# Layer 3's spreading matrix: from a comparison of positions to a turned selection

## The chip, the cores and the metric

The kernel runs on one core of one Trainium2 chip. The time is device microseconds of one execution. Three runs of the kernel before took 1780.59, 1781.38 and 1783.02 us, so the median is 1781.38 us. Beside these there is one profiled execution, from which the trace is taken; it has its own time.

## The reference

A graph of 3327 nodes with 512 features goes through four layers. Each layer adds its input to its output and normalises the rows. The change touches the fourth, called layer 3, an attention layer with 4 heads of 128:

```python
h = jnp.einsum('nf,hfo->hno', x, hamilton)
f_src = jnp.einsum('hno,ho->hn', h, a_src)
f_dst = jnp.einsum('hno,ho->hn', h, a_dst)
e = jax.nn.leaky_relu(f_src[:, :, None] + f_dst[:, None, :], ALPHA)
e = jnp.where((adj > 0)[None, :, :], e, NEG_INF)
attn = jax.nn.softmax(e, axis=-1)
h_prime = jnp.einsum('hnm,hmo->hno', attn, h)
out = jnp.transpose(h_prime, (1, 0, 2)).reshape(N, -1)
return jax.nn.elu(out)
# and around it
x = _layernorm(x + _L3_gnn_ref(x, adj, L3_gnn_W, L3_gnn_a), axis=-1)
```

The adjacency is sparse except for its first rows and columns, so the kernel works on lists of edges.

## The kernel before, in words

The nodes lie in 26 blocks of 128 rows. For each block from 1 to 25 the kernel has a list of the edges that end in it, sorted so that the edges of one row lie side by side. A list is cut into chunks of 128 edges ("places"). Block 1 has 15 chunks, later blocks have fewer (6 around block 11, 5 from block 15, 4 from block 23), 165 in all. The edges from the first 128 nodes are left out of the lists and added per block as a dense product, called the column here.

One to four chunks make a group, and the function `group` handles one group. It is a Python generator, and each `yield` ends one of its stages. In layer 3, before the change, its stages are:

1. POOL starts one indirect transfer per chunk (L1005), which gathers 128 rows of 2,080 bytes from the table in device memory into a ring of 27 chunk places. ACT zeroes the weights of places that don't exist (L1253) and computes |2 x place - middle| per row (L1267, "far").
2. DVE compares it with the row's number of edges (L1277). The result "ds" is the spreading matrix: 128 rows by 128 places per chunk, 1 where the place belongs to the row.
3. PE multiplies ds with the rows' own scores, in three parts (L1291, into "pg"), so that every place gets the score of its row.
4. DVE adds the gathered score and takes the maximum (L1304, L1306, "sc"); ACT takes the exponential twice (L1307, L1308) and turns the kept selection of layer 2 from 8 bits into f32 (L1312, "sel"): 128 places by 128 rows per chunk, 1 where the place belongs to the row.
5. DVE multiplies the gathered rows by the weights (L1315).
6. PE adds sel times these rows to the block's sums in PSUM (L1334). With the last chunk goes the column's product (L1331).

The list `sall` keeps the selection that layer 2 built for all its groups, and `kept` returns a group's part of it. It is there for every block that layer 3 handles in groups. In layer 0 it isn't.

From layer 1 on the order of the instructions on every engine is the order in which the program issues them. In layer 3 that order comes from this loop:

```python
for k, item in enumerate(groups(pools[0], range(1, NB))):
    if item[4] == 0:
        ends.add(g3.column(item[0], fin))
    work.add(g3.group(item, pools, accs, layer3, sall))
    both()
```

`both` is one step: first every live group runs its next stage, the oldest first; then every live generator of the list `ends` does, the oldest first. `ends` holds two kinds. A column is added when its block's first group is added:

```python
nc.sync.dma_start(up, ...)                     # L1366
for _ in range(4):
    yield
for h in range(H):
    nc.scalar.activation(up[:, h, :], ..., AF.Relu, ...)   # L1371, ACT
yield
nc.vector.scalar_tensor_tensor(up, up, ...)    # L1373, DVE
```

So four Relus on ACT come four steps after the block's first group has been started, and DVE's product "upc" comes one step later. Three buffers hold "upc". The other kind, `layer3_end`, is added when a block's last chunk has been summed. One step later it divides by the sum of the weights (DVE "rden", L1481 and L1482; ACT "h", four instructions, L1485) and takes an exponential (ACT "e", L1495). In the step after that DVE finishes the row (L1497, L1498) and takes its moments (L802, L804), and ACT takes a logarithm and an exponential of the variance ("r", L828 and L829). In the third DVE refines it (L835 to L837, "nm" in L856), ACT scales the row ("o", L857), and SP stores it (L770).

Of the kernel before, what the change touches and what calls it, by code (L numbers as in the profile page):

```python
# [8 lines left out]
F32 = mybir.dt.float32  # L9
BF16 = mybir.dt.bfloat16  # L10
# [6 lines left out]
I16 = mybir.dt.int16  # L17
AF = mybir.ActivationFunctionType
ALU = mybir.AluOpType
AX = mybir.AxisListType  # L20
PSUM = bass.MemoryType.PSUM
DRAM = bass.MemoryType.DRAM

P = 128
# [513 lines left out]
GROUP = 4  # L538
# [93 lines left out]
def sparse_path(ctx, tc, flag_i, x, adj, l0_w, l0_a1, l0_a2, l1_w_self, l1_b_self, l1_w_nb, l1_b_nb,  # L632
# [13 lines left out]
    nc = tc.nc  # L646
# [12 lines left out]
    def pool_in(lay, name, bufs=1, **kw):  # L659
        return lay.enter_context(tc.tile_pool(name=name, bufs=bufs, reuse_waits="tile", **kw))  # L660
# [38 lines left out]
    dgs = keep.tile([P, NL, 2], F32, name="dgs")  # L699
# [10 lines left out]
    def iota(name, n, dtype, step, base, mult, pool=const):  # L710
        t = pool.tile([P, n], dtype, name=name)
        nc.gpsimd.iota(t, pattern=[[step, n]], base=base, channel_multiplier=mult,
                       allow_small_or_imprecise_dtypes=True)
        return t
# [3 lines left out]
    ident16 = const.tile([P, P], BF16, name="ident16")  # L718
# [3 lines left out]
    place = iota("place", LMAX * P, I16, 1, 0, 0)  # L722
# [45 lines left out]
    def store(dst_d, b, t, shift=0):  # L768
        for p0, p1 in rows_of(b):
            nc.sync.dma_start(dst_d[shift + b * P + p0:shift + b * P + p1, :], t[p0:p1])  # L770
# [83 lines left out]
    def scaled_by_act(o, y, fin, mv, rs):  # L854
        nm = fin.tile([P, 1], F32, name="nm")
        nc.vector.scalar_tensor_tensor(nm, mv[:, 0:1], -1.0, rs, ALU.mult, ALU.mult)  # L856
        nc.scalar.activation(o, y, AF.Identity, bias=nm, scale=rs)  # L857
# [127 lines left out]
    def groups(ring, blocks=range(NB), whole=False):  # L985


        for b in blocks:
            at = 0
            for l in lists[b]:  # L990
                c0, end = 0, l.L if whole else l.up
                while c0 < end:
                    left = end - c0
                    g = -(-left // -(-left // GROUP))
                    if ring.ahead() < g:
                        g = ring.ahead()
                    yield b, l, c0, g, at
                    c0 += g
                    at += g
# [10 lines left out]
    def kept(sall, b, at, g):  # L1010

        if sall is None or b == 0:
            return None
        at += spot[b]
        lo, t = next((lo, t) for lo, t in reversed(sall) if lo <= at)
        return t[:, at - lo:at - lo + g, :]
# [9 lines left out]
    class Gat:  # L1026
# [199 lines left out]
        def close_first(self, pool, ps, mean):  # L1226
# [11 lines left out]
            for s in range(2):  # L1238
                nc.tensor.matmul(self.acc[s], lone, G[0:1, s * hh:(s + 1) * hh, :], start=False, stop=True)

        def group(self, item, pools, accs, done, sall=None):

            b, l, c0, g, at = item
            ring, sp, pacc, pone = pools
            H, OUT, M = self.H, self.OUT, self.M
            hh = H // 2
            whole = self.k == 0
# [5 lines left out]
                nc.scalar.copy(G[p0:p0 + 32, g - 1].rearrange("p (h m) -> p h m", m=M)[:, :, OUT:],  # L1253
                               zeros[p0:p0 + 32, :2 * H].rearrange("p (h s) -> p h s", s=2))

            na = min(g, max(0, l.up - c0))
            nb = min(g, max(0, l.down - c0)) if whole else g
            far = sp.tile([P, GROUP * P], I16, name="far")
            parts = [(far, 0, 0, na), (far, 1, na, g if whole else na)]
            if nb < na:  # L1260
                more_far = sp.tile([P, 2 * P], I16, name="far1")
                assert na - nb <= 2
                parts.append((more_far, 1, nb, na))
            for t, k, q0, q1 in parts:
                if q0 < q1:
                    o = t[:, q0 * P:q1 * P] if t is far else t[:, :(q1 - q0) * P]
                    nc.scalar.activation(o, place[:, (c0 + q0) * P:(c0 + q1) * P], AF.Abs,  # L1267
                                         bias=l.nmid[:, k:k + 1], scale=2.0)
            yield
            have = kept(sall, b, at, g)  # L1270
            ds = sp.tile([P, GROUP * P], BF16, name="ds")
            for t, k, q0, q1 in parts:
                o, dk = ds[:, q0 * P:q1 * P], dgs[:, l.at, k:k + 1]
                if t is not far:
                    nc.vector.scalar_tensor_tensor(o, t[:, :(q1 - q0) * P], dk, o, ALU.is_lt, ALU.add)
                elif q0 < q1:
                    nc.vector.tensor_scalar(o, t[:, q0 * P:q1 * P], dk, None, ALU.is_lt)  # L1277
            yield

            pg = pone.tile([P, 512], F32, name="pg")  # L1280
# [3 lines left out]
            for c in range(g):  # L1284
# [5 lines left out]
                for k in range(3):  # L1290
                    nc.tensor.matmul(po, ds[:, c * P:(c + 1) * P], self.own[:, k, :, b],  # L1291
                                     start=k == 0, stop=k == 2)
            S = sp.tile([P, GROUP, P], F32, name="sel")
            if have is None:
                turned = pg[:, 256:].bitcast(BF16)
# [27 lines left out]
            for c in range(g):  # L1323
# [9 lines left out]
                for s in range(2):  # L1333
                    nc.tensor.matmul(accs[b][s], S[:m, c, :], G[:m, c, s * hh * M:(s + 1) * hh * M],  # L1334
                                     start=at + c == 0, stop=last)
# [188 lines left out]
    lay, listlay, wxlay = ExitStack(), ExitStack(), ExitStack()  # L1524
# [16 lines left out]
    with ExitStack() as pro:  # L1541
# [81 lines left out]
        ready, whole = -1, True  # L1623
# [194 lines left out]
    def both():  # L1818
        work.step()
        ends.step()  # L1820
# [9 lines left out]
    with ExitStack() as lay:  # L1830
# [6 lines left out]
        sp = pool_in(lay, "l1s", 3)  # L1837
# [120 lines left out]
    with ExitStack() as lay:  # L1958
        fin = pool_in(lay, "l2f", 2)
        sp = pool_in(lay, "l2s", 1)  # L1960
# [5 lines left out]
        g3 = Gat("g3", t3_d, H3, OUT3, w3, 1)  # L1966
# [75 lines left out]
    with ExitStack() as lay:  # L2042
        pools = (Ring(H3 * (OUT3 + 2), rows, extra), pool_in(lay, "l3s", 3),
                 pool_in(lay, "l3pa", 2, space=PSUM), pool_in(lay, "l3p1", 3, space=PSUM))
        fin = pool_in(lay, "l3f", 2)

        def layer3(b, acc):
            ends.add(layer3_end(b, acc))

        def layer3_end(b, acc):  # L2050
            yield
            e, mv, rs = yield from g3.summed(fin, acc, xres[b])
            o = fin.tile([P, D], F32, name="o")
            scaled_by_act(o, e, fin, mv, rs)
            store(out, b, o)

        def verdict():

            yield
            bad = fin.tile([P, 4, NL], F32, name="bad")  # L2060
            nc.vector.memset(bad, 0.0)
            nc.vector.tensor_tensor(bad[:, 0, :], deg[:, 1:], cnt, ALU.not_equal)
            used = fin.tile([P, 3, NL], F32, name="used")
            room = fin.tile([P, 3, NL], F32, name="room")
            nc.vector.tensor_add(used[:, 1:], starts.rearrange("p l s -> p s l"), dgs.rearrange("p l s -> p s l"))
            nc.vector.tensor_add(used[:, 0], used[:, 1], used[:, 2])
            for ls in lists:
                for l in ls:
                    for k, n in enumerate((l.room, l.near, l.far)):
                        nc.gpsimd.memset(room[:, k, l.at:l.at + 1], float(n))  # L2070
            yield
            nc.vector.tensor_tensor(bad[:, 1:], used, room, ALU.is_gt)
            tot = fin.tile([P, 2], F32, name="tot")
            nc.vector.tensor_reduce(tot[:, 0:1], bad, AX.XY, ALU.add)
            nc.vector.tensor_reduce(tot[:, 1:2], spread, AX.X, ALU.add)
            nc.vector.tensor_add(tot[:, 0:1], tot[:, 0:1], tot[:, 1:2])
            yield
            pt = pools[3].tile([P, 512], F32, name="pg")
            nc.tensor.matmul(pt[0:1, 0:1], tot[:, 0:1], ones[:, 0:1], start=True, stop=True)
            nc.vector.tensor_copy(flag_i, pt[0:1, 0:1])  # L2080

        ends.add(g3.open_column(fin))
# [5 lines that stand above are left out]
            if k == 6:  # L2088
                ends.add(layer3_end(0, bias1))
            if k == 12:  # L2090
                ends.add(verdict())
        while work.live or ends.live:
            both()


@with_exitstack
def kernel(ctx: ExitStack, tc: tile.TileContext, *args):


    nc = tc.nc  # L2100
    pool = ctx.enter_context(tc.tile_pool(name="flagp", bufs=1))
    flag_i = pool.tile([1, 1], I32, name="flag_i")
    sparse_path(tc, flag_i, *args)
    again = nc.values_load(flag_i[0:1, 0:1], min_val=0, max_val=1 << 20)
    with tc.If(again > 0):
        general_path(tc, *args)
# [30 lines left out]
```

## Time and profile before

| what | value |
|---|---|
| runs shown, median of three | 1781.38 us (1780.59 to 1783.02) |
| the profiled execution, its own time | 1689.52 us |
| the profiled span, first to last instruction | 1687.8 us |
| mean granted TensorE clock | 0.957 |
| gathers of layer 3 on POOL | 165, from 1418.1 to 1635.3 us |
| multiplication of the first and of the last group (L1315) | 1429.2 and 1662.5 us |
| busy from 1460 to 1660 us (200 us) | PE 167.1, DVE 180.8, ACT 155.3, POOL 135.2 us |

Times within the profile are counted from the span's start. A line of the timeline gives the start, the duration, the engine, the line of the kernel, the operation, what it writes and reads, and how many instructions are merged; a bracket at its end gives the engine's idle time before it and what ended that. The chain lists the work that determined the end, in order of time.

### The profile page before, as it was taken

What the parts mean: (1) busy time and instruction counts of PE and PEld (TensorE: products, weight loads), DVE (VectorE), ACT (ScalarE), POOL (GpSimd) and SP (SyncE); (2) the same over time, 40 slices, a digit from 0 to 9 for tenths busy, and PEclk for the clock granted to TensorE, in tenths of its full rate; (3) what the DMA queues carried; (4) which work ended last, traced back from release to release, by engine and by line L of the source; (5) the groups of instructions that cost most, each with busy time, mean ns of one, the idle gap of its engine ahead of it and who ended that gap; (6) DMA issues with size and microseconds to landing.
All of it is one profiled execution on the core that took longest, in us unless ns stands there. A gap on an engine that the chain in (4) does not pass through costs nothing. (4 is left out here: it accounts for less than half of the span.)

```text
span 1687.8 us, 24368 instructions
## 1 busy us (share of the span) xinstructions
PE 1490.9 (88%) x7298; PEld 994.6 (59%) x7298; DVE 1220.4 (72%) x3289; ACT 874.4 (52%) x2921; POOL 767.4 (45%) x904
## 2 busy tenths in 40 slices
PE   5979987989999989889999999787999996888884
PEld 3756655656666767445555555433566664777663
DVE  7998979988668789316556677547666644789996
ACT  5889856666666768312112221112444444568885
POOL 3000076564554620065445445047777402777750
PEclk9989989999999999879999999899999997999998
DMA  8787787776664542198888889168998613888871
GB/s 258 241 285 248 233 256 252 236 205 197 190 189 148 182 121 89 46 390 327 292 311 302 318 300 342 72 207 289 300 322 296 219 38 114 228 232 253 253 225 46
DMA packets 130401, 381.98 MB, mean 226 GB/s; under 512 B 22037, under 2 KB 36477, under 8 KB 130259
## 3 DMA queue, kind: packets, MB, share of 16 engines
q0 software_dynamic: 67696, 252.97, 46.7%
q1 hardware_dynamic: 62563, 127.35, 22.3%
q8 instruction: 60, 0.98, 0.2%
q14 instruction: 82, 0.67, 0.1%
HBM read 331.89 MB, written 48.37 MB: 225 GB/s over the span
## 5 line engine op out<-in xcount | busy, mean ns | idle before, releaser
L1005 POOL DMA_INDIRECT gl<-t_d,idx x270 | 274.2, 1015 | 221.9 <-DMA e_d<-es 80.6
L1005 POOL DMA_INDIRECT gt<-t_d,idx x201 | 203.6, 1013 | 345.2 <-DVE cand L921 198.0
L1334 PE MATMUL acc<-gt,sel 128*128 128x264 f32 (+3 forms) x804 | 208.7, 405 | 3.7 <-issue 1.8
L797 PE MATMUL po<-wn,xt 128*128 128x512 f32 x416 | 195.5, 613 | 11.6 <-ACT vc L963 4.9
L1005 POOL DMA_INDIRECT gm<-t_d,idx x136 | 136.5, 1004 | 137.9 <-PE acc L1810 87.8
L1334 PEld LDWEIGHTS acc<-gt,sel 128*128 128x128 f32 (+3 forms) x804 | 151.0, 197 | 39.6 <-issue 13.4
L1334 PE MATMUL acc<-gl,sel 128*128 128x260 f32 (+3 forms) x544 | 140.8, 405 | 27.1 <-issue 14.9
L797 PEld LDWEIGHTS po<-wn,xt 128*128 128x128 f32 x416 | 79.4, 196 | 96.7 <-issue 77.5
L1334 PEld LDWEIGHTS acc<-gl,sel 128*128 128x128 f32 (+3 forms) x544 | 102.6, 198 | 44.5 <-issue 15.6
L1315 DVE TENSOR_TENSOR gt<-gt,pg 128x1536 f32<-128x1536 f32 (+3 forms) x63 | 116.3, 1847 | 13.6 <-ACT sel L1310 13.4
L1042 PE MATMUL po<-gt,xt 128*128 128x268 f32 x416 | 111.4, 410 | 15.5 <-ACT xt L789 11.6
L785 ACT COPY xt<-pt 128x512 f32<-128x512 f32 x81 | 46.8, 588 | 132.1 <-PE pt L782 121.8
L1810 PE MATMUL acc<-gm,selr 128*128 128x512 f32 (+4 forms) x324 | 107.9, 457 | 4.5 <-DMA gm<-t_d,idx 4.1
L909 DVE MAX8 cand<-val 128x8 f32<-128x464 uint16 (+32 forms) x184 | 107.5, 619 | 0.0
L1042 PE MATMUL po<-w,xt 128*128 128x262 f32 x416 | 99.3, 392 | 5.2 <-ACT xt L789 3.9
L1042 PEld LDWEIGHTS po<-gt,xt 128*128 128x128 f32 x416 | 75.6, 195 | 34.3 <-ACT xt L789 15.5
L1267 ACT ACTIVATE far<-place,nmids 128x128 int16<-128x128 int16 (+3 forms) x167 | 88.3, 545 | 13.5 <-DVE ds L1277 12.9
L797 PE MATMUL po<-wl,xt 128*128 128x512 f32 x208 | 93.4, 594 | 0.7 <-ACT xt L785 0.7
L797 PE MATMUL po<-wx,xt 128*128 128x512 f32 x208 | 93.5, 594 | 0.0
L1042 PEld LDWEIGHTS po<-w,xt 128*128 128x128 f32 x416 | 78.9, 192 | 23.1 <-ACT xt L789 5.8
L782 PE MATMUL pt<-s_ident,xres 128*128 128x128 f32 x500 | 78.8, 287 | 14.2 <-DVE xres L852 10.0
L881 ACT ACTIVATE m<-ab 128x1664 bf16<-128x1664 int32 x50 | 80.1, 1603 | 16.8 <-DMA ab<-in_adj_dram 12.5
(372 smaller groups left out, 3225.6 us busy)
## 6 DMA issues: line engine op xcount, KB each, us to landing
ab<-in_adj_dram SPq DMA_DIRECT2D x25, 832.0 KB
ab<-in_adj_dram SPq DMA_DIRECT2D x25, 831.5 KB
t_d<-t SPq DMA_DIRECT2D x25, 512.0 KB
gm<-t_d POOLq DMA_DIRECT2D x25, 512.0 KB
t_d<-t SPq DMA_DIRECT2D x25, 384.0 KB
t_d<-tg SPq DMA_DIRECT2D x25, 264.0 KB
gd<-t_d SPq DMA_DIRECT2D x25, 264.0 KB
t_d<-tg SPq DMA_DIRECT2D x25, 260.0 KB
```

The source lines that it names most:

```text
L782: nc.tensor.transpose(pt[:, c, :], src[:, c * P:(c + 1) * P], ident)
L785: nc.scalar.copy(xt, pt)
L797: nc.tensor.matmul(po, xt[:, c, :], w[:, c], start=c == 0, stop=c == DC - 1)
L881: nc.scalar.activation(m, ab[s], AF.Sign, accum_out=half[:, s, b:b + 1])
L909: nc.vector.max(out=cand[:, s, :], in_=val[:, cuts[s]:cuts[s + 1]])
L1005: nc.gpsimd.indirect_dma_start(out=t[:m, c, :], out_offset=None, in_=table[:, :], in_offset=bass.IndirectOffsetOnAxis(ap=l.idx[:m, c0 + c: ...
L1042: nc.tensor.matmul(pw[s], xt[:, c, :], self.w[:, c, s, :], start=c == 0, stop=c == DC - 1)
L1267: nc.scalar.activation(o, place[:, (c0 + q0) * P:(c0 + q1) * P], AF.Abs, bias=l.nmid[:, k:k + 1], scale=2.0)
L1315: nc.vector.tensor_mul(Gc[:, :, :OUT], Gc[:, :, :OUT], w[:, :g].rearrange("p c (h o) -> p (c h) o", o=1).to_broadcast([P, g * H, OUT]))
L1334: nc.tensor.matmul(accs[b][s], S[:m, c, :], G[:m, c, s * hh * M:(s + 1) * hh * M], start=at + c == 0, stop=last)
L1810: nc.tensor.matmul(accs[b], chosen, parts[:, k * D:(k + 1) * D], start=at + c + k == 0, stop=k == top and at + c == n - 1)
```

## The change

In layer 3 the spreading matrix is no longer computed from the positions. PE multiplies each chunk of the kept selection (8 bits, as stationary operand) with the 128 x 128 identity, which turns it, into a PSUM tile "pd" of a new pool with one buffer. ACT copies that tile into ds as bf16. The absolute value on ACT and the comparison on DVE are left out. The group has seven stages instead of six: gather; turn on PE; copy on ACT; then stages 3 to 6 as before. The old code goes into a function of its own, `spread_own`, which layer 0 still runs, in the same order as before.

```diff
+        def spread_own(self, sp, l, c0, g, whole):
             na = min(g, max(0, l.up - c0))
             nb = min(g, max(0, l.down - c0)) if whole else g
...
                     nc.scalar.activation(o, place[:, (c0 + q0) * P:(c0 + q1) * P], AF.Abs,
                                          bias=l.nmid[:, k:k + 1], scale=2.0)
             yield
-            have = kept(sall, b, at, g)
-            ds = sp.tile([P, GROUP * P], BF16, name="ds")
+            self.ds = ds = sp.tile([P, GROUP * P], BF16, name="ds")
...
                     nc.vector.tensor_scalar(o, t[:, q0 * P:q1 * P], dk, None, ALU.is_lt)
+
+        def group(self, item, pools, accs, done, sall=None):
...
+            have = kept(sall, b, at, g)
+            if have is not None:
+                yield
+                turned = self.around.tile([P, 512], F32, name="pd")
+                for c in range(g):
+                    nc.tensor.matmul(turned[:, c * P:(c + 1) * P], have[:, c, :], ident16, start=True, stop=True)
+                yield
+                ds = sp.tile([P, GROUP * P], BF16, name="ds")
+                nc.scalar.copy(ds[:, :g * P], turned[:, :g * P])
+            else:
+                yield from self.spread_own(sp, l, c0, g, whole)
+                ds = self.ds
             yield
...
+        g3.around = pool_in(lay, "l3p0", 1, space=PSUM)
```

More of the change, by code (lines that the diff above doesn't have):

```diff
@@ L1239, in close_first @@
                 nc.tensor.matmul(self.acc[s], lone, G[0:1, s * hh:(s + 1) * hh, :], start=False, stop=True)
[L1241 to L1247, printed above, removed]
-            total = (chunks_all if whole else chunks_of)[b]
-            G = gather(ring, self.table, l, c0, g, whole)
-            m = l.places(c0 + g - 1, whole)
-            for p0 in range(m, P, 32):
-                nc.scalar.copy(G[p0:p0 + 32, g - 1].rearrange("p (h m) -> p h m", m=M)[:, :, OUT:],
-                               zeros[p0:p0 + 32, :2 * H].rearrange("p (h s) -> p h s", s=2))
+        def spread_own(self, sp, l, c0, g, whole):
             na = min(g, max(0, l.up - c0))
@@ L1277, in group @@
                     nc.vector.tensor_scalar(o, t[:, q0 * P:q1 * P], dk, None, ALU.is_lt)
+        def group(self, item, pools, accs, done, sall=None):
+            b, l, c0, g, at = item
+            ring, sp, pacc, pone = pools
+            H, OUT, M = self.H, self.OUT, self.M
+            hh = H // 2
+            whole = self.k == 0
+            total = (chunks_all if whole else chunks_of)[b]
+            G = gather(ring, self.table, l, c0, g, whole)
+            m = l.places(c0 + g - 1, whole)
+            for p0 in range(m, P, 32):
+                nc.scalar.copy(G[p0:p0 + 32, g - 1].rearrange("p (h m) -> p h m", m=M)[:, :, OUT:],
+                               zeros[p0:p0 + 32, :2 * H].rearrange("p (h s) -> p h s", s=2))
+            have = kept(sall, b, at, g)
[10 more added lines that the diff above has]
+                ds = self.ds
             yield
```

## The prediction

> **What bounds the kernel now.** I read the page's shares first, then layer 3 in stretches of 20 us, then the chain, then the timeline of single blocks. The page, and two of the stretches (busy us and instruction count of PE, PEld, DVE, ACT, POOL; granted clock; DMA share; GB/s):
>
> ```profile
> PE 1490.9 (88%) x7298; PEld 994.6 (59%) x7298; DVE 1220.4 (72%) x3289; ACT 874.4 (52%) x2921; POOL 767.4 (45%) x904
> ...
> 1600.00:1620.00 20.00, 16.30 (x111) 13.24 (x110) 18.75 (x47) 17.90 (x58) 15.43 (x16) 1.00 0.84 244
> 1640.00:1660.00 20.00, 15.98 (x104) 12.41 (x104) 18.18 (x48) 16.44 (x52) 0.00 (x0) 1.00 0.22 67
> ```
>
> Over the whole span PE looks like the bound; in layer 3 DVE (91 to 94%) and ACT (82 to 90%) are the fullest. POOL issues a gather every 1.25 us (16 in 20 us) until 1635 and is done 27 chunks before the consumer. Two regimes follow. In blocks 1 to 5 a group's product on DVE starts 4.7 to 11.9 us after its last gather was issued, at the low end waiting for data. From block 10 (1539.8) the distance is 8.3 us and it grows to 28: here the gathers are ahead and something else sets the pace. The chain says what, for one block of 3 + 2 chunks:
>
> ```profile
> 1623.12 0.51 ACT far L1267
> 1623.63 0.70 ACT o L857
> 1624.33 1.03 ACT h L1485 x4
> 1625.39 0.64 ACT e L1495
> 1626.05 0.70 DVE h L1497
> 1626.78 0.70 DVE e L1498
> 1627.50 0.70 DVE st L802
> 1628.36 1.16 DVE gl L1315
> 1631.28 0.51 ACT far L1267
> ```
>
> It is a ring through ACT and DVE, once per block, closed by sc, max, the weights and sel. No engine is full for lack of speed alone: each waits for the other inside a fixed order. I call the step in which DVE multiplies a block's first group the first step, the one with its second group the second step. The timeline of both:
>
> ```profile
> 1618.77 1.63 ACT L1371 ACTIVATE upc<-upc,low,rcol 128x128 f32<-128x128 f32 x4
> 1620.06 0.18 DVE L804 BATCH_NORM_AGGREGATE mv<-st 128x2 f32<-128x6 f32 x1
> 1620.31 0.28 ACT L828 ACTIVATE r<-mv,s_eps 128x1 f32<-128x1 f32 x1
> ...
> 1621.98 0.51 ACT L1312 ACTIVATE sel<-salla 128x384 f32<-128x384 fp8e4 x1
> 1622.49 0.61 ACT L1253 COPY gl<-zeros 32x8 f32<-32x8 f32 x3
> 1623.12 0.51 ACT L1267 ACTIVATE far<-place,nmids 128x256 int16<-128x256 int16 x1
> 1623.53 0.80 ACT L857 ACTIVATE o<-e,nm,rs 128x512 f32<-128x512 f32 x1
> ```
>
> The four Relus for the column stand in the first step, and end just when ACT's next work ("r") gets its input from DVE: they are free. In the second step ACT goes from sel to o, h and e without a gap, and DVE then waits for e.
>
> **What the Trainium skill says.** "PSUM — Partial Sum Buffer", section "Engine vs sequencer instructions": ScalarE and VectorE work their queues strictly in order. The trace agrees: where Relus stand ahead of o, o waits for them (shown below). "ScalarE: Activation LUTs", section "What ACT_TABLE_LOAD costs": an activation takes 186 ns plus 0.833 ns per element, 280 with a bias pointer, and neighbours overlap by 93 ns. The trace agrees: sel of 384 takes 506 ns, far of 384 takes 602.
>
> **The change part by part.**
>
> Removed from DVE: the comparison, in the window from 1450 us 9.4 + 3.9 + 2.5 + 0.5 = 16.3 us in 50 groups, 0.33 us each. Removed from ACT: far, 0.60 us for 384, 0.50 for 256. Added on ACT: a copy out of PSUM. The nearest row is layer 0's cast of the turned tile from PSUM, 467 ns at 128x384, and 588 ns for f32 at 128x512; the skill's price for 384 is 506, less 93 of overlap 413. I take 0.42 us from start to start for 384 (ends: 0.33 and 0.51). ACT alone would thus win about 0.1 us per group. Added on PE: one 128 x 128 turn per chunk. Layer 0's turns of the same size take 0.35 us for three in a row, so 0.12 each; 8-bit weights load in 98 ns in layer 2, so they are no dearer. For 165 chunks that is 19 us on an engine with 3 to 4 us idle in each 20. Sending the transfers costs the same: 165 gathers, in the same order on POOL, with no new DMA on any queue.
>
> The added stage is what I think decides. A group's product now comes five steps after its start, not four, while the column still counts four steps from that start to its Relus. So everything that is issued by count from the start moves one step earlier against the products, the sums and the row ends. Most blocks have two groups, so the Relus move from the first step, where they cost nothing, into the second, and there they stand ahead of o, h and e, because the column is older in the list than the row ends. DVE's upc moves into the first step, ahead of h, where DVE waits for e anyway: free. ACT's zeroing of absent places moves from the second step into the first: 0.2 to 0.6 us off the ring. Of SP's queue: the load of the next column waits for the sum that frees its buffer, now one step later relative to it; three steps (about 13 us) are left to the Relus against a few for the load, and the stores behind it on SP have two buffers: no cost.
>
> The ring before, start to start, from h at 1617.88: DVE h 0.73, e 0.73, st 0.72, mv 0.10, product of two chunks 1.11, sc 0.22, max to the weights 0.26 (1621.75), weights 0.23, sel 0.51, zeros 0.63, far 0.41, o 0.71, h 1.15, e 0.66 = 8.17 (next h at 1626.05). Over blocks 15 to 22 the mean is (1647.5 - 1583.8) / 8 = 7.97, since blocks without zeros are held by DVE's nm instead. After: without zeros and far, with the copy 0.42 and the Relus 1.54 (1618.77 to 1620.31): 8.17 - 1.04 + 1.96 = 9.1. For 3 + 3 chunks the product adds 0.54 less 0.09 of shorter waits: 9.55. For 4 + 3, sel and copy add 0.2: 9.75; for 4 + 4 the product adds 0.55: 10.3.
>
> Summed by first products (L1315): blocks 6 to 9 took 1503.97 to 1539.78 = 35.8, after 10.3 + 3 x 9.75 = 39.5: +3.7. Blocks 10 to 12 took 25.6, after 3 x 9.55 = 28.6: +3.0. Block 13 has three groups and block 14 two, 18.4 together; one of the two meets the new order: +1.0. Blocks 15 to 22: 8 x (9.1 - 7.97) = +9.0. Blocks 23 and 24, 14.9: +1.1 each, +2.2. Blocks 1 to 5 and the 25 us after the last product: 0. Sum +18.9. The span goes from 1687.8 to about 1707, the profiled execution from 1689.5 to about 1708. The runs shown are 92 us above the profiled one; nothing in layer 3 says that this part changes, so the median goes from 1781.4 to about 1800.
>
> What the kernel before shows of this order: around block 13, with its three groups, Relus fall into the step of o:
>
> ```profile
> 1580.57 0.16 DVE L856 SCALAR_TENSOR_TENSOR nm<-mv,rs 128x1 f32<-128x1 f32 x1
> 1580.61 0.60 ACT L1267 ACTIVATE far<-place,nmids 128x384 int16<-128x384 int16 x1
> 1581.12 1.63 ACT L1371 ACTIVATE upc<-upc,low,rcol 128x128 f32<-128x128 f32 x4
> 1582.66 0.80 ACT L857 ACTIVATE o<-e,nm,rs 128x512 f32<-128x512 f32 x1
> ```
>
> nm is done at 1580.73, and o starts at 1582.66, when the Relus end.
>
> The new waits: PE's turn waits for ACT's copy of the group before (one buffer), and that stands behind the weights and sel. Behind the turn on PE stand the sum of an older group and the scores of the next. In the first step the copy comes after e, some 6.2 us after the ring's max. PE then turns (0.35), sums three chunks (2.87), makes the scores (0.3) and is done at about 9.8; the addition that needs them comes at 9.1 + 2.7 = 11.8. About 2 us of cover; without it each us of delay costs a us per block. PE's own work is 5 x 0.96 + 1.05 + 0.7 + 0.6 = 7.1 of 9.1; for 4 + 4 it is 10.7, 0.4 above the ring, in one block.
>
> **The rivals.** (1) DVE relief wins, ending faster. For: DVE is at 94%, and 16.3 us leave it. If the Relus keep cover, the ring loses far minus copy (0.1 to 0.2) and part of the zeros, about 0.25 us in 16 blocks: -4, 1777. Decided by where the Relus stand: it holds if they end before mv. Against: the count of four steps is not changed. (2) PE becomes the bound: turn after copy after sel, one buffer, and the sums behind it late for the addition. From 2 us more delay than worked out above, each further us goes onto the block; with 0.5 us in 20 blocks, 1810. Against: the cover above. (3) Half of it: up to block 12 the gathers hide the longer ring, since there 7 to 8 chunks take 8.75 to 10 us of POOL. Then 1.0 + 9.0 + 2.2 = +12, 1793. Against: the distance to the gathers grows already from block 9. (4) Nothing moves, within 3 us of 1781: the Relus in the second step are made up by a DVE that is free earlier. Against: DVE waits for e there.
>
> **How the numbers follow.** Relus on the ring 0.58, half of it 0.14, PE bound 0.15, relief 0.08, nothing 0.05. The likeliest gives 1800, its own range 1794 to 1808 (copy 0.33 to 0.51 is +-2 us over 20 blocks, three-group blocks and the tail +-3). The 8-in-10 range reaches to the half case and PE's: 1787 to 1812. About 0.2%, 3.6 us, is what a measurement of this kernel can tell from no change. Faster 0.08, same 0.05, slower 0.87.
>
> **What would show it.** Right: in blocks 15 to 22 the Relus follow the copy and o follows the Relus, DVE waits over 1 us per block for e, and first products lie about 9.1 us apart; DVE's share from 1460 to 1660 falls below 85%. Wrong: the Relus still end before r; or PE's sums wait for the turn and sc waits for PE's scores (rival 2); or the multiplications up to block 12 keep their times (rival 3).

## The result and the profile after

| | before | after |
|---|---|---|
| median of 15 runs each | 1782.22 us (1773.4 to 1790.63) | 1794.8 us (1787.45 to 1802.38) |
| ratio | 1 | 1.0075, 95% interval 1.006 to 1.009 |
| predicted | 1781.4 | 1800, range 1787 to 1812 |

The change makes the kernel slower by 12.6 us between the medians; 18.9 were predicted. The profiled execution of the kernel after took 1793.12 us, that of the kernel before 1689.52. These two profiles don't belong side by side: in the runs of this result the kernel before itself takes 1782 us, while in the runs of every experiment below it takes 1690.5 to 1691.8. So both kernels were profiled again in the experiments, and what is subtracted below comes from that pair.

The page of the kernel after, engines and their shares:

```profile
PE 1515.9 (85%) x7463; PEld 1011.0 (56%) x7463; DVE 1207.3 (67%) x3232; ACT 865.2 (48%) x2921; POOL 758.6 (42%) x904
```

PE has the 165 turns more (7298 to 7463), and DVE has 57 instructions less, one for each of the 57 groups. ACT keeps its count: 57 copies took the place of 57 absolute values. The busy time of layer 3, first of the kernel before, profiled again (busy us and count of PE, PEld, DVE, ACT, POOL; clock; DMA share; GB/s):

```profile
1460.00:1660.00 200.00, 168.19 (x1106) 138.48 (x1107) 180.75 (x458) 154.77 (x475) 136.38 (x210) 0.96 0.79 230
```

and then of the kernel after, profiled in the same way:

```profile
1460.00:1660.00 200.00, 160.95 (x1167) 135.21 (x1166) 155.09 (x370) 134.75 (x434) 134.41 (x210) 0.96 0.77 225
```

DVE goes from 90.4 to 77.5% and ACT from 77.4 to 67.4%. A part of that is only that fewer blocks fall into the 200 us; the rest is relief, and both engines are idle longer. The chain of the kernel after shows what they wait for, for one block of 3 + 2 chunks (from the profile of 1793.12 us; "..." marks lines left out):

```profile
1704.17 0.46 ACT ds L1288
1704.63 1.55 ACT upc L1385 x4
1706.18 0.70 ACT o L857
...
1708.59 0.70 DVE h L1511
```

Where the ring before had far (0.51) and then o, there are now the copy (0.46) and four Relus (1.55). The timeline of the same step:

```profile
1704.17 0.46 ACT L1288 CAST ds<-pd 128x384 bf16<-128x384 f32 x1
1704.53 1.65 ACT L1385 ACTIVATE upc<-upc,low,rcol 128x128 f32<-128x128 f32 x4
1706.08 0.80 ACT L857 ACTIVATE o<-e,nm,rs 128x512 f32<-128x512 f32 x1
1708.59 0.69 DVE L1511 SCALAR_TENSOR_TENSOR h<-h,xres 128x512 f32<-128x512 f32 x1 [1.61 <-ACT e L1509]
```

The Relus follow the copy, o follows the Relus, and DVE's h then waits 1.61 us for e. What that comes to is in the view of waits, DVE alone, from 1431 us, just before the first product of layer 3, to the end (who waits for whom, us in total, times, longest). The kernel before, profiled again:

```profile
DVE h L1497 <- ACT e L1495: 8.4, 11, 2.2
DVE bad L2072 <- POOL room L2070: 2.8, 1, 2.8
```

The kernel after, profiled again:

```profile
DVE h L1511 <- ACT e L1509: 32.1, 22, 2.2
DVE bad L2087 <- POOL room L2085: 8.1, 1, 8.1
```

DVE waits 23.7 us more for e, twice as often, and 5.3 us more in a single place ("bad", which the section on the second cause takes up). Over the same stretch DVE's busy time falls from 218.8 to 205.7 us, by 13.1, and all its waits rise from 27.6 to 58.3 us, by 30.7, of which these two are 29.0. The difference, 17.6 us, is nearly the whole loss of 18.9 in the span: the relief came, and more than twice as much came in waits.

The sum by first products of the same two profiles (spans 1690.9 and 1709.8):

| stretch | before, us | after, us | measured difference | predicted |
|---|---|---|---|---|
| first product at | 1432.0 | 1431.2 | -0.8 | 0 |
| blocks 1 and 2 | 35.2 | 35.6 | +0.4 | 0 |
| blocks 3 to 5 | 39.2 | 44.7 | +5.5 | 0 |
| blocks 6 to 9 | 36.5 | 35.7 | -0.8 | +3.7 |
| blocks 10 to 12 | 25.7 | 29.0 | +3.3 | +3.0 |
| blocks 13 and 14 | 18.4 | 19.9 | +1.5 | +1.0 |
| blocks 15 to 22 | 63.7 | 71.1 | +7.4 | +9.0 |
| blocks 23 and 24 | 14.9 | 17.3 | +2.4 | +2.2 |
| after the last product | 25.2 | 25.3 | +0.1 | 0 |
| sum | | | +19.0 | +18.9 |

From block 10 on the terms agree with their prediction (14.6 against 15.2). Before it they don't: 5.5 us come up in blocks 3 to 5, where nothing was expected, and blocks 6 to 9, where 3.7 were expected, are 0.8 shorter. That the totals agree is partly luck: two errors of 5.5 and 4.5 us with opposite signs. The experiments have to explain both.

### The profile page after: what moved, and what is told of

Read it like the earlier page. It is cut to its first block, busy times and chain, and to the rows that moved or that the text cites. A ratio compares the mean times of both kernels' runs of the same rounds, so it can differ in the third digit from the quotient of the medians.

```text
span 1791.3 us, 24613 instructions
## 1 busy us (share of the span) xinstructions
PE 1515.9 (85%) x7463; PEld 1011.0 (56%) x7463; DVE 1207.3 (67%) x3232; ACT 865.2 (48%) x2921; POOL 758.6 (42%) x904
## 5 line engine op out<-in xcount | busy, mean ns | idle before, releaser
L1005 POOL DMA_INDIRECT gl<-t_d,idx x270 | 266.6, 987 | 283.7 <-DMA e_d<-es 79.3
L797 PE MATMUL po<-wn,xt 128*128 128x512 f32 x416 | 197.4, 618 | 13.9 <-ACT xt L785 5.4
L1348 PE MATMUL acc<-gl,sel 128*128 128x260 f32 (+3 forms) x544 | 144.9, 412 | 4.6 <-DVE upc L1387 2.9
L1042 PEld LDWEIGHTS po<-w,xt 128*128 128x128 f32 x416 | 77.5, 189 | 25.0 <-ACT xt L789 7.4
L782 PE MATMUL pt<-s_ident,xres 128*128 128x128 f32 x500 | 78.7, 286 | 15.2 <-DVE xres L852 10.2
L782 PEld LDWEIGHTS pt<-s_ident,xres 128*128 128x128 f32 x500 | 61.3, 147 | 39.0 <-issue 25.0
```

Source lines behind the costliest of these rows:

```text
L782: nc.tensor.transpose(pt[:, c, :], src[:, c * P:(c + 1) * P], ident)
L797: nc.tensor.matmul(po, xt[:, c, :], w[:, c], start=c == 0, stop=c == DC - 1)
L1005: nc.gpsimd.indirect_dma_start(out=t[:m, c, :], out_offset=None, in_=table[:, :], in_offset=bass.IndirectOffsetOnAxis(ap=l.idx[:m, c0 + c: ...
L1042: nc.tensor.matmul(pw[s], xt[:, c, :], self.w[:, c, s, :], start=c == 0, stop=c == DC - 1)
```

## The experiments

The main theory is that of the prediction: the added stage puts the Relus ahead of o, h and e. The rivals are PE (turns, and one buffer for them), and the stage itself by some other way. Every ratio is against the kernel before on the same chip, with its 95% interval in brackets. The runs come from four chips, on which the kernel before takes 1690.5 to 1691.8 us. Block times are from one profile each, so small differences between them prove little alone. Every edit that moves the Relus also moves DVE's product upc, which comes one step behind them.

### Both kernels again

> The kernel before, unchanged, for a second profile: the first profiled execution took 1689.5 us, 92 us less than the median of the runs. All theories expect an execution near 1781 us. If the missing 92 us are stalls of all engines that lie outside the fixed order of layer 3, the first products of blocks 15 to 22 are again 8.0 us apart, and the rest differs from the first profile by gaps of 10 us and more in which every engine stands still.

> The changed kernel, unchanged, beside the kernel before on whatever chip this is. On a chip where the kernel before takes near 1690 us, where gathers come every 1.25 us and blocks 6 to 12 aren't held up by data, theory: the sum of my prediction counts in full, +16 to +19 us, ratio 1.0095 to 1.011 (the empty stage alone made 1.0107). On a chip where the kernel before takes near 1780 us, the gathers hide the part of blocks 6 to 12: ratio 1.007 to 1.008 again. Rival (the turn and its buffer give some of it back or cost something of their own): the ratio differs from that of the empty stage by more than 0.002.

The kernel before took 1692.65 us in a single run (span 1690.9), where 1781 had been expected. The kernel after took 1711.58 us, ratio 1.0106 (1.0082 to 1.013): 20.2 us more than the kernel before beside it. The 92 us between the runs shown and the first profile are thus not a property of layer 3's order, since the kernel before has them in one set of runs and not in the other.

### Relus one step later, in the kernel after

```diff
-            for _ in range(4):
+            for _ in range(5):
```

> The changed kernel with the column's Relus five steps after the block's start instead of four, so that they stand in the first step again. Theory of the Relus: they end before the logarithm's input is there, o follows the copy directly, a block of 3 + 2 chunks takes 8.9 - 1.55 + 0.3 (DVE's side of the ring becomes the longer one) = 7.5 to 7.9 us, and the time is below that of the kernel before: 1770 to 1780 us, ratio 0.994 to 0.999. Theory of PE's turn and its single buffer: nothing of that is changed, so the time stays near 1795 us, ratio 1.007.

1688.45 us, ratio 0.9989 (0.9982 to 0.9997). One number undoes the whole loss. Below, this is the kernel with count 5. Timeline of ACT, from a second step into the first step of the next block:

```profile
1619.14 0.51 ACT L1326 ACTIVATE sel<-salla 128x384 f32<-128x384 fp8e4 x1
1619.55 0.46 ACT L1288 CAST ds<-pd 128x384 bf16<-128x384 f32 x1
1620.11 0.81 ACT L857 ACTIVATE o<-e,nm,rs 128x512 f32<-128x512 f32 x1
...
1624.01 1.65 ACT L1385 ACTIVATE upc<-upc,low,rcol 128x128 f32<-128x128 f32 x4
1625.57 0.28 ACT L828 ACTIVATE r<-mv,s_eps 128x1 f32<-128x1 f32 x1
```

Now o follows the copy, and the Relus stand ahead of r again, as before the change. Blocks 15 to 22 lie 7.70 us apart. DVE's wait for e, 1.61 us with the Relus in the way, is 0.29 here in the block from 1617.3.

### Relus one step earlier, in the kernel before

```diff
-            for _ in range(4):
+            for _ in range(3):
```

> The kernel before with the Relus three steps after the block's start instead of four: they stand in the second step, ahead of o, h and e; no turn, no copy, no added stage. Theory of the Relus: a block of 3 + 2 chunks takes 8.0 to 8.2 plus 1.55 = 9.5 to 9.7 us (the zeroing stays in the ring), +1.5 us in some 16 blocks, 1800 to 1808 us, ratio 1.011 to 1.015. Theory of PE's turn: as the kernel before, 1782 us, ratio 1.000.

1711.42 us, ratio 1.013 (1.0111 to 1.0149). Here there is no turn, no copy and no added stage, only the Relus in the second step:

```profile
1626.70 0.40 ACT L1253 COPY gl<-zeros 32x8 f32<-32x8 f32 x2
...
1627.53 1.63 ACT L1371 ACTIVATE upc<-upc,low,rcol 128x128 f32<-128x128 f32 x4
1629.07 0.80 ACT L857 ACTIVATE o<-e,nm,rs 128x512 f32<-128x512 f32 x1
```

Its blocks 15 to 22 take 9.34 us each (9.5 to 9.7 had been expected), 0.46 more than after the change. Part of that is the zeroing of absent places (0.40 in this step): with six stages it still stands in the second step, ahead of the Relus. The next run has far and the comparison too, but not the zeroing in this step, and takes 8.94.

### An empty stage, in the kernel before

```diff
+            if not whole:
+                yield
             na = min(g, max(0, l.up - c0))
```

> The kernel before with one empty stage after the gather: seven stages, the spreading matrix still from positions. Theory of the Relus: the added stage alone moves them into the second step, so nearly all of the loss is there: ring 8.92 plus 0.05 to 0.15 (absolute value instead of copy) = about 9.0 us, 1793 to 1798 us, ratio 1.006 to 1.009. Theory of PE's turn: no turn, so as before, 1782 us or, with more time for the gathers, a little less.

1710.21 us, ratio 1.0107 (1.0089 to 1.0126): a stage that does nothing costs the same as the change, and more than the 1.006 to 1.009 that had been expected of it.

```profile
1628.37 1.63 ACT L1373 ACTIVATE upc<-upc,low,rcol 128x128 f32<-128x128 f32 x4
1629.91 0.80 ACT L857 ACTIVATE o<-e,nm,rs 128x512 f32<-128x512 f32 x1
...
1632.40 0.69 DVE L1499 SCALAR_TENSOR_TENSOR h<-h,xres 128x512 f32<-128x512 f32 x1 [1.22 <-ACT e L1497]
```

Relus, o and DVE's wait for e stand as in the kernel after, at 8.94 us per block. DVE's upc isn't the cause: in both kernels it is done before this wait begins, and DVE then stands still for 1.2 and 1.6 us.

### Every turn done twice

```diff
-                for c in range(g):
+                for c in (*range(g), *range(g)):
```

> The changed kernel with every turn on PE done twice into the same place: PE's part of the change is doubled, 165 more products of 0.11 to 0.12 us, some 19 us of PE time. Theory of the Relus: PE has about 2 us of cover per block of 3 + 2 chunks, so blocks 15 to 22 stay 8.9 us apart and the time is that of the changed kernel within 0.2%, up to 3 us more from the blocks of 4 + 3 and 4 + 4 chunks. Theory of PE and its single buffer: what the turn costs is on the path, +0.6 us per block of 3 + 2 chunks, 12 us or more over the changed kernel.

1712.55 us, ratio 1.0113 (1.0089 to 1.0138), not to be told from the 1.0106 of the kernel after on the same chip. Twice PE's turns, and the blocks stay at 8.88 us. The timeline of PE in this kernel shows why:

```profile
1612.43 0.49 PE L1285 MATMUL pd<-ident,sallb 128*128 128x128 bf16 x6 [1.38 <-ACT ds L1288]
...
1615.45 0.31 PE L1305 MATMUL pg<-g3own,ds 128*128 128x8 bf16 x6
```

PE waits for the copy, which frees the one buffer; then it turns, sums three chunks and makes the scores, which are done at 1615.76. DVE, which has two products to do, adds them at 1617.99, 2.2 us later (2.4 in the kernel after: 1612.97 and 1615.37). Doubling the turns takes 0.2 us of a cover that nothing else needs. This takes the second rival out.

### The turn in the gather's stage

```diff
             if have is not None:
-                yield
                 turned = self.around.tile([P, 512], F32, name="pd")
```

> The changed kernel with the turn in the same stage as the gather: six stages as before, so the column's count of four fits again, and the turn and the copy are all that is left of the change. Theory of the Relus: the loss is gone; the zeroing is back in the second step (0.4 to 0.6 us in the ring of blocks with absent places), so a block of 3 + 2 chunks takes 7.7 to 8.0 us, ratio to the kernel before 0.997 to 1.001. Theory of PE's turn: turn, copy and one buffer are all there, ratio 1.007 or more.

1688.35 us, ratio 0.9985 (0.9973 to 0.9996). The kernel has turn and copy, but six stages, and the Relus are where they were; 7.98 us per block.

### The empty stage with the Relus moved along

```diff
+            if not whole:
+                yield
...
-            for _ in range(4):
+            for _ in range(5):
```

> The kernel before with the empty stage after the gather and the Relus five steps after the block's start: the fourth corner beside the changed kernel, the changed kernel with five steps, and the empty stage with four. What turn and copy are worth in place of absolute value and comparison once the Relus are off the ring: theory, DVE's comparison is then on the ring again (0.25 us per block) and far replaces the copy, so blocks of 3 + 2 chunks take 7.8 to 8.0 us against 7.60, ratio to the kernel before 0.998 to 1.002, that is 2 to 5 us more than with the turn. If the Relus weren't the cause, this would be near 1.0107 like the empty stage with four.

1693.21 us, ratio 1.0004 (0.9991 to 1.0018), 7.86 us per block. With this the runs fill a table (ratios to the kernel before):

| | Relus in the first step | Relus in the second step |
|---|---|---|
| six stages, comparison | 1 (before) | 1.013 |
| seven stages, comparison | 1.0004 | 1.0107 |
| six stages, turn and copy | 0.9985 | |
| seven stages, turn and copy | 0.9989 | 1.0106 (after) |

The columns differ by 1.0 to 1.3%, whatever stands in the rows. Turn and copy in place of the comparison are worth -0.15% in six stages (0.9973 to 0.9996, so 0.7 to 4.6 us of 1690). In seven stages the medians differ by as much with the Relus in the first step (0.9989 against 1.0004, overlapping intervals, two chips) and not at all with them in the second. So the change's own idea pays about 2.5 us, and the step it was given costs some 20.

### Relus behind the row ends

```diff
+        columns = Stages()
...
-                ends.add(g3.column(item[0], fin))
+                columns.add(g3.column(item[0], fin))
...
             both()
+            columns.step()
```

> The changed kernel with the columns in a list of their own, which is stepped after the row ends: the same seven stages, the same count of four, the Relus still in the second step, but behind e instead of ahead of o. Theory of the Relus: what costs is their place ahead of o, h and e, not the step as such; behind e they run while DVE does h, e, st and mv (2.3 us), so a block of 3 + 2 chunks goes from 8.9 back to 7.6 to 7.8 us, ratio to the kernel before 0.998 to 1.001 on a chip where that takes near 1690 us. If the added stage costs in another way (PE's order, later sums), nothing is won: 1.0106 again.

1695.12 us, ratio 1.0025 (1.0014 to 1.0036): most of the loss is gone, and 0.25% stays. The timeline of the second step, the Relus behind e at last, and DVE's upc:

```profile
1611.05 0.63 ACT L1509 ACTIVATE e<-h 128x512 f32<-128x512 f32 x1
1611.58 1.63 ACT L1385 ACTIVATE upc<-upc,low,rcol 128x128 f32<-128x128 f32 x4
...
1613.99 0.67 DVE L1387 SCALAR_TENSOR_TENSOR upc<-upc,col 128x512 f32<-128x512 f32 x1
```

The stage is kept, the count is kept, only the place in the queue is another: it is the place that costs. The blocks take 8.03 us instead of 8.88. That is more than the 7.70 with count 5 and the 7.6 to 7.8 expected. DVE shows what is left: upc has moved as well and now stands between the moments and the next block's product, 0.6 us from start to start, and DVE still waits 0.70 for e in most blocks (0.29 with count 5).

### One more step between e and the rest of the row

On the kernel with count 5:

```diff
             nc.scalar.activation(e, hq, AF.Exp)
             yield
+            if self.k:
+                yield
```

> The changed kernel with the Relus five steps after the start, and one more step between the exponential of a row end and DVE's part of it, so that the ring through ACT and DVE no longer closes within one block. If the ring of 7.6 us still sets the pace in the changed kernel with five steps, blocks of 3 + 2 chunks come down to DVE's own work of 7.4 to 7.5 us, and the ratio to the kernel before to 0.996 to 0.998; if DVE's work is already the bound, nothing changes: 0.9985 to 0.999, or a little more for the later ends.

1694.1 us, ratio 1.0018 (1.0008 to 1.0028), so slower than without the edit (0.9989). Blocks 15 to 22 take 8.53 us. DVE no longer waits for e, but for something else:

```profile
1627.96 0.69 DVE L1387 SCALAR_TENSOR_TENSOR upc<-upc,col 128x512 f32<-128x512 f32 x1 [1.20 <-ACT upc L1385]
```

DVE comes to upc 1.2 us before ACT has ended the Relus for it, and h stands behind upc in its queue. With the wait for e taken off the ring, the wait for the Relus is on it. The expectation had named a gain or next to no change; that the edit makes a loss was not foreseen.

## The second cause: a wait of DVE behind POOL's queue

The 5.5 us of blocks 3 to 5 are not made by the Relus: in the experiments' profiles these blocks take 42.6 to 45.1 us in every kernel with seven stages and the verdict at its old place (45.1 even with count 5), and 38.2 to 39.6 in the kernels with six. With the 13th group the program issues a final check of the lists, the generator `verdict`: 75 small memsets on POOL ("room"), and one step later a comparison on DVE ("bad") that needs them. The comparison in the kernel before, profiled again:

```profile
1486.78 0.24 DVE L2072 TENSOR_TENSOR bad<-used,room 128x75 f32<-128x75 f32 x1 [2.77 <-POOL room L2070]
```

Memsets and comparison in the kernel after, profiled again:

```profile
1483.67 2.21 POOL L2085 MEMSET room<- 128x1 f32 x75
1485.91 0.24 DVE L2087 TENSOR_TENSOR bad<-used,room 128x75 f32<-128x75 f32 x1 [8.07 <-POOL room L2085]
```

The memsets stand behind the gathers of the groups issued so far, one each 1.25 us, and end within 1 us of each other in both kernels (1485.9 here, 1486.7 in the kernel before). But with a product that comes five steps after its group's start, not four, DVE has one product less ahead of "bad": 11, where the kernel before has 12. So it arrives at 1477.8 instead of 1484.0 and waits 8.07 us instead of 2.77. The difference, 5.3 us, is nearly all of the +5.5 of the table. The expectation below names 8.1 to 8.6 and 2.8 us for this wait; over all profiles of the experiments it is 8.1 to 9.3 with seven stages and 0.9 to 2.8 with six.

The wait also changes blocks 6 to 9. Matching the 165 gathers to the products in order, a group's product in these blocks comes 7.3 to 9.3 us after its last gather was issued in the kernel before, and 11.0 to 14.9 us in the kernel after: there the gathers got ahead during the wait. From first product to first product these blocks take (us):

| | block 6 (4 + 4 chunks) | blocks 7 to 9 (4 + 3 each) |
|---|---|---|
| kernel before | 8.9 | 27.6 |
| kernel after | 6.9 | 28.8 |
| kernel after with count 5 | 6.8 | 25.2 |
| predicted for after | 10.3 | 29.25 |

In blocks 7 to 9 the long ring is there as predicted. Against count 5, which has the same distances (10.5 to 15.0), it costs 3.6 us; against the kernel before only 1.2, because that one runs at 9.2 us per block, near the 8.75 that seven gathers take. Block 6 is where the prediction is off: it follows a block of three groups, and in the trace of the kernel after its Relus end before r (1511.98) and o follows later without them, so the long ring isn't in it. In the kernel before DVE waits 1.65 us there for gathered data.

> The changed kernel with the Relus five steps after the start, and the verdict on the lists' sizes put in at group 50 instead of group 12 (75 small memsets on POOL, and a comparison on DVE that waits for them). All seven-stage kernels showed DVE standing still for 8.1 to 8.6 us at that comparison, six-stage ones for 2.8 us. Theory: at group 50 POOL is 10 chunks and more ahead, so DVE doesn't wait, and the memsets no longer hold up gathers that are waited for; blocks 3 to 5 take 35 to 39 us instead of 45, the ratio to the kernel before goes from 0.9989 to 0.993 to 0.996, the fastest so far. If the lost time of blocks 3 to 5 is only shifted (the gathers then set the pace of blocks 6 to 12), the ratio stays at 0.998 to 0.999.

```diff
-            if k == 12:
+            if k == 50:
                 ends.add(verdict())
```

On the kernel after with count 5 this gives 1685.71 us, ratio 0.9959 (0.9943 to 0.9975), the fastest of all, and below both kernels. The wait is gone:

```profile
1633.64 0.23 DVE L2087 TENSOR_TENSOR bad<-used,room 128x75 f32<-128x75 f32 x1
```

Blocks 3 to 5 fall from 45.1 to 36.0 us; blocks 6 to 9 rise from 32.0 to 38.0, because with products 5.3 to 9.1 us behind the gathers these set the pace again. Net 3.1 us, of the 5 us that the ratios differ by (0.30% of 1690). Blocks 15 to 22, where the check now falls, take 1.6 us more. The two profiles are of the slowest of nine runs here and the fastest of 22 there, so the rest of the difference can't be placed.

> The kernel before with the verdict at group 50 instead of group 12. Its wait there was 2.8 us, so less is to be won than with seven stages: ratio 0.996 to 0.999. If the seven-stage kernels' 45 us for blocks 3 to 5 came of the verdict, the gain here is smaller than that from 0.9989 to the other run's ratio; if it came of the added stage in another way, both gain the same.

The same edit in the kernel before: 1692.18 us, ratio 0.9997 (0.9987 to 1.0007): nothing, where 0.996 to 0.999 had been expected. Blocks 3 to 5 win 3.9 us (35.3), blocks 6 to 9 give 1.7 back (38.2), and blocks 15 to 22, where the check now falls, another 2.5 (66.2). In the two kernels blocks 3 to 9 then take 73.5 and 74.0 us, near the 70.0 that their 56 gathers take at 1.25. Both have a short ring; the long ring with the late check was not run.

## Why the prediction was right, point by point

**The mechanism was right.** The step "everything that is issued by count from the start moves one step earlier" carried the forecast. The order copy, Relus, o, the wait of over 1 us for e in most blocks and DVE below 85% (77.5) were all found; the empty stage, the count of 3 and the count of 5 show that the order alone makes or unmakes the loss. The Trainium skill's statement that ScalarE works its queue strictly in order ("PSUM — Partial Sum Buffer", "Engine vs sequencer instructions") is what the runs show: with the Relus ahead of o, o starts at their end (1706.08, while they end at 1706.18); behind e they cost ACT the same 1.6 us and the blocks 0.85 us less.

**The ring was nearly right.** 9.1 us were predicted for blocks 15 to 22, 8.88 were measured, so this term is 7.4 and not 9.0. The copy takes 0.46 us (0.36 from start to start in this step; 0.42 had been taken), the Relus 1.55 (1.54). The skill's price for an activation of 384 elements, 506 ns ("ScalarE: Activation LUTs", "What ACT_TABLE_LOAD costs"), is a little high for this copy out of PSUM, and right for sel.

**The zero costs.** "DVE's upc: free" and "SP: no cost" saw nothing against them in the chain. PE's cover was put at about 2 us and is 2.4. The turn takes 0.33 us for three chunks (0.35).

**What failed: "Blocks 1 to 5: 0".** The prediction followed each work that is issued by count from a group's start and belongs to the groups or columns. It did not follow the verdict, which is issued by the loop's own count: its DVE instruction also moved against the products, and DVE now reaches it before POOL is done. This costs 5.3 us where it falls.

**What failed: "blocks 6 to 9 [...] +3.7".** Block 6 was put at 10.3 us with the Relus ahead of o; they aren't there, and it took 6.9. The prediction's two regimes were blocks 1 to 5 and from block 10 on; it gave the long ring to blocks 6 to 9 all the same. The two failures nearly cancel: blocks 3 to 9 grow by 4.7 us, where 3.7 were predicted.

**What failed: the step from the profile to the runs.** With the sentence "nothing in layer 3 says that this part changes" the whole 18.9 was added to the median of 1781.4. In the runs of the result only 12.6 were added (10.7 to 16.0 by the interval), though the median stays within the range.

**The rivals.** Relief of DVE without the Relus on the ring is real and small: -0.15%, about 2.5 us, where 4 had been worked out; it needs count 5 or the early turn. PE as the bound is excluded by the doubled turn. The third rival, half of it hidden by the gathers, gave 1793, and the median of 1794.8 lies nearer to it than to 1800. In the experiments' runs its sum of 12 does not hold (+20.2 us, interval 13.9 to 22.0), but its mechanism is seen in blocks 7 to 9. In the runs of the result it may hold: in their one trace, that of the kernel after, the first product comes 50 us later than in the kernel after profiled again, blocks 1 and 2 take 60.0 us instead of 35.6, and there are stretches in which DVE stands still:

```profile
1504.18 0.21 DVE L1318 TENSOR_TENSOR sc<-pg,gl 128x32 f32<-128x32 f32 x1 [20.48 <-issue]
```

From 1490 to 1500 us PE and ACT have no work either, while POOL starts a gather every 1.25 us. In this trace DVE does not wait at "bad": it gets there at 1557.8, and the memsets ended at 1544.2. So the second cause is shown for the experiments' runs and not for those of the result. No trace of the kernel before exists from such runs, so why the change costs 12.6 us there and 20.2 in the others stays open, and the two intervals overlap. What makes the 92 us stays open too.

## What to carry to other kernels

In a pipeline whose order comes from counted steps, a new stage is never only the work in it: list everything that counts steps from elsewhere (columns, row ends, checks at a fixed index), and for each say ahead of which instruction it now stands in its engine's queue, and behind which it waits in another's. Test such a change with its empty stage alone, and give the counters the same extra step before judging the idea itself; here that turned +1.06% into -0.11%. A product's distance from its last gather tells whether a stretch can show a longer ring at all.

## What the runs showed that was not expected

- An empty `yield` costs 1.07% (1.0089 to 1.0126), without one instruction more or less.
- 75 memsets of 2.21 us together can hold DVE for 2.77 or 8.07 us. They stand behind the gathers on POOL and end at nearly the same time in both kernels; what differs is when DVE gets to the comparison.
- The same kernel before took 1782 us in one set of runs and 1690.5 to 1691.8 in the others, 5% apart, while the ratio of after to before only went from 1.0075 to 1.0106, with overlapping intervals (1.006 to 1.009 and 1.0082 to 1.013).
